# Accumulators of idle streams lent to the running ones in a four-layer graph-attention kernel

## The chip, the cores and the metric

The kernel runs on one core of a Trainium2 chip. The metric is the device time of one execution in microseconds (us); lower is better. Before the change the median of three runs is 2951.32 us (2948.66 to 2954.25).

## What is computed

The input `x` holds 32 batches of 512 nodes with 256 features, and `adj` is one 512 x 512 graph for all. Four residual layers follow each other, each with a layer norm and a relu ahead of it. Cut to what matters:

```python
def gat(h, W, a_i, a_j, alpha, mask):            # one attention
    Wh  = h @ W
    e   = leaky_relu((Wh @ a_i)[:, :, None] + (Wh @ a_j)[:, None, :], alpha)
    att = softmax(where(mask, e, -inf), axis=2)
    return att @ Wh

for layer in (0, 1, 2, 3):
    h = relu(layernorm(x))
    # 0: x += elu(gat(h, W0, alpha=0.2))           masked
    # 1: x += relu(gat(h, W1, alpha=0.01))         masked
    # 2: x += elu(gat with 4 heads of 64 features) masked
    # 3: o = relu(h @ mlp1_w + b1)                 512 features
    #    o = elu(elu(gat(o, W_fc, 0.2, no mask))) + o
    #    r = relu(o @ mlp2_w + b2)                 256 features
    #    x += relu(elu(elu(gat(r, W_hand, 0.2))) + r)
```

All of it is in fp32. The exponentials of a leaky relu of a sum factor into products, so the kernel needs no exponential of a 512 x 512 matrix: it builds `w = max(row, column) * mask` on VectorE and multiplies values that were scaled before.

## The kernel before

The 32 batches run in `NS = 4` streams: stream i works on batches i, i + 4, i + 8 and so on, one after another. A stream is a Python generator (`stream`, `batch`, `layer0` to `layer3`). Each time it has recorded a piece of work it yields the time at which its next piece may begin. The loop at L748 to L762 always runs the generator with the smallest time, so that pieces of the four streams are interleaved in the recorded program. Stream i begins `LEAD = 75` planned microseconds after stream i - 1, and each ends when its last batch is done; so only at the beginning and at the end are there fewer than four at work. A fifth generator, `setup`, prepares the mask and the projected weight columns in the same loop (L750 to L755) with the banks of the last stream.

After the recording, a scheduler puts the instructions of each engine in an order, planning with the dependences and with the buffers that each tile may use. Every engine then runs its list in that order. So a different supply of buffers can change the order on all engines, and not only waits.

TensorE's results land in the 8 accumulator banks of PSUM, each 128 x 512 fp32. `bank()` (L74) hands them out: the tag is `b` and the number of the current stream, with `8 // NS = 2` buffers per tag. `turn[0]` is the current stream, set by the loop (L756). During `setup` it is stream 3, but the mask's four transposed blocks go round the streams 3, 2 and 1 (L209). A tile of a tag waits until the tile two before it on that tag has been read by ScalarE (ACT) or VectorE (DVE).

All matmuls go through `matmul` (L66) and all transposes through `transpose` (L70), so the profile shows these two lines; the tile names tell which part it is. The users of `bank()` that the change and the prediction touch:

- `project` (L107): the projected columns of a weight (`WFC`, `WHA` and so on). Transposes into one bank, an ACT copy to `wT` (L114), matmuls of 3 columns into a second bank, and a DVE copy (L120).
- `values` (L301): four blocks of `h @ W`, each read by two ACT instructions (L312 and L313, or L315 and L318 with `both` of L317 between).
- `weights` (L336): four transposes of a column, then four DVE instructions `w` (L346, or L352 without mask).
- `averages` (L390): four matmuls `v,w` of 257 columns, a reciprocal on DVE (L380), and ACT reads (L414 and L415, L433, L692 and L693).
- `project_half` (L512): a block of the 512-wide attention's values, read by ACT (L521 and L522).
- `sort_attend` (L556): the unmasked attention by sorting, with scatters (L600), reloads (L607), prefix sums on DVE (L618 to L639) with small matmuls `before` and `after` between, a table to DRAM (L640), and gathers into two buffers `g` (L648) that L663, L667 and L668 read. `mlp_in` (L712) transposes each result `y` and adds it (L719).
- `attend` (L524): the same attention by matmuls, for batch 31 alone.
- `norm` (L256): statistics (L262, L263) and the normalised `xn` (L269 or L273), which `turn_pair` transposes and ACT copies to `hT` (L283). `add_elu` (L396) ends layers 0 and 2 with L398 and L399.

Of the kernel before, what the change touches and what calls it, by code (L numbers as in the profile page):

```python
# [19 lines left out]
FP = mybir.dt.float32  # L20
# [8 lines left out]
P = 128  # L29
# [6 lines left out]
def fast(ctx, tc, flag, x, adj, w0, a0, w1, a1, w2, a2, mlp1_w, mlp1_b, mlp2_w, mlp2_b,  # L36
         w_fc, a_fc, w_hand, a_hand, out):
    nc = tc.nc
    B, N, F = x.shape
# [6 lines left out]
    NS = 4  # L46
# [6 lines left out]
    psum = ctx.enter_context(tc.tile_pool(name="psum", bufs=1, space=bass.MemoryType.PSUM))  # L53
    dram = ctx.enter_context(tc.tile_pool(name="dram", bufs=1, space=bass.MemoryType.DRAM))

    turn = [0]
# [11 lines left out]
    def transpose(p, x, i, tied=False):  # L68
        spent[0] += 2 * P
        instruction = nc.tensor.transpose(p, x, i)  # L70
        if tied:
            tc.keep_in_program_order(instruction)

    def bank():  # L74
        return psum.tile([P, N], FP, tag=f"b{turn[0]}", name="b", bufs=8 // NS)


    nc.scalar.preload_act_table_set("natural_log_exp_and_others")
# [28 lines left out]
    def project(dst, block, k, a_cols):  # L107

        ft, n = a_cols.shape[1], a_cols.shape[2]
        p = bank()  # L110
        for f in range(ft):
            transpose(p[:, f * P:(f + 1) * P], block(k, f), ident)
        wT = work.tile([P, N], FP, tag="y", name="wT", bufs=3)
        nc.scalar.copy(wT[:, :ft * P], p[:, :ft * P])  # L114
        q = bank()
        for f in range(ft):
            matmul(
                q[:, :n], wT[:, f * P:(f + 1) * P], a_cols[:, f, :], start=(f == 0), stop=(f == ft - 1)
            )
        nc.vector.tensor_copy(dst, q[:, :n] if len(dst.shape) == 2 else q[:, :n].rearrange("p (h c) -> p h c", c=3))  # L120
# [79 lines left out]
    def setup():  # L200
# [7 lines left out]
        for j in range(NT):  # L208
            turn[0] = NS - 1 - j % (NS - 1)  # L209
            p = bank()  # L210
            for t in range(NT):
                transpose(p[:, t * P:(t + 1) * P], own[:, t, j * P:(j + 1) * P], ident, j + t == 0)
            nc.scalar.copy(maskT[:, j, :], p)
# [534 lines left out]
    while ready:  # L748
        i = min(ready, key=ready.get)
        if i == NS:  # L750
            turn[0] = NS - 1
            ready[i] += 4.0
            if next(early, early) is early:
                del ready[i]
            continue  # L755
        turn[0], spent[0] = i, 0.0  # L756
        begun[0] = ready[i]
        wait = next(streams[i], None)
        if wait is None:
            del ready[i]  # L760
        else:
            ready[i] = wait  # L762

# [409 lines left out]
@with_exitstack  # L1173
def kernel(ctx: ExitStack, tc: tile.TileContext, *args):
    nc = tc.nc
    keep = ctx.enter_context(tc.tile_pool(name="keep", bufs=1))
    flag = keep.tile([1, 1], I32, name="flag")
    fast(tc, flag, *args)
    bad = nc.values_load(flag[0:1, 0:1], min_val=0, max_val=1)
    with tc.If(bad > 0):  # L1180
        general(tc, *args)
# [27 lines left out]
```

## Time and profile before

| | |
|---|---|
| median of three runs | 2951.32 us |
| profiled execution | 2955.39 us, span 2953.7 us |
| TensorE (PE) busy | 2870.6 us, 97% |
| weight loads (PEld) | 2329.4 us, 79% |
| VectorE (DVE) busy | 2224.6 us, 75% |
| ScalarE (ACT) busy | 1538.9 us, 52% |
| GpSimd (POOL) busy | 497.2 us, 17% |
| mean TensorE clock granted | 0.994 |
| instructions | 43083 |
| DMA | 270.89 MB, 92 GB/s |

Busy times are sums over an engine's instructions. Matmuls are pipelined and their ends are modelled, so a busy TensorE need not be one at its peak; an fp32 matmul of L66 shows as two passes, a transpose of L70 as one. Lines of a timeline give the start in us, the length, the engine, the line and operation, the tiles (written <- read), and in brackets how long the engine was idle before and what released it.

### The profile page before, as it was taken

What the parts mean: (1) busy time and instruction counts of PE and PEld (TensorE: products, weight loads), DVE (VectorE), ACT (ScalarE), POOL (GpSimd) and SP (SyncE); (2) the same over time, 40 slices, a digit from 0 to 9 for tenths busy, and PEclk for the clock granted to TensorE, in tenths of its full rate; (3) what the DMA queues carried; (4) which work ended last, traced back from release to release, by engine and by line L of the source; (5) the groups of instructions that cost most, each with busy time, mean ns of one, the idle gap of its engine ahead of it and who ended that gap; (6) DMA issues with size and microseconds to landing.
All of it is one profiled execution on the core that took longest, in us unless ns stands there. A gap on an engine that the chain in (4) does not pass through costs nothing.

```text
span 2953.7 us, 43083 instructions
## 1 busy us (share of the span) xinstructions
PE 2870.6 (97%) x15177; PEld 2329.4 (79%) x15177; DVE 2224.6 (75%) x5674; ACT 1538.9 (52%) x3918; POOL 497.2 (17%) x509
## 2 busy tenths in 40 slices
PE   7999999999999999999999999999999999999998
PEld 5778888778887877888778888778878778887765
DVE  4578878778878777878778777787777788777763
ACT  3445555554555555555545555545555555555544
POOL 0011122111122121121111121111121111221120
PEclk9999999999999999999999999999999999999999
DMA  3033233233232332233332232222232322332330
GB/s 93 12 100 95 83 98 115 82 99 98 83 101 96 99 101 91 85 106 94 101 94 87 87 115 92 96 97 91 87 116 90 98 94 86 94 115 76 98 108 16
DMA packets 193150, 270.89 MB, mean 92 GB/s; under 512 B 16992, under 2 KB 156062, under 8 KB 192928
## 3 DMA queue, kind: packets, MB, share of 16 engines
q1 hardware_dynamic: 163168, 169.76, 18.4%
q0 software_dynamic: 29760, 98.30, 10.2%
q8 instruction: 123, 2.02, 0.3%
q14 instruction: 99, 0.81, 0.1%
HBM read 152.62 MB, written 115.39 MB: 91 GB/s over the span
## 4 chain that ended last, share of the span: by engine, by line
PE 80%; DVE 12%; ACT 5%; issue 1%; DMA 1%; POOL 0%; SPq 0%; POOLq 0%; ACTq 0%; DVEq 0%
PE b L66 72%; PE b L70 7%; DVE st L262 3%; DVE xn L273 1%; DVE xn L269 1%; DVE sums L634 1%; ACT v L318 1%; DVE sums L625 1%; DVE x L399 1%; ACT rs L265 1%; DVE y L398 1%; DVE mv L263 1%; DVE y L703 1%; ACT y L498 1%; ACT q L497 0%
## 5 line engine op out<-in xcount | busy, mean ns | idle before, releaser
L66 PE MATMUL b<-v,w 128*128 128x65 f32 (+1 forms) x7232 | 1221.6, 321 | 11.0 <-DVE w L346 8.5
L66 PEld LDWEIGHTS b<-v,w 128*128 128x128 f32 x7232 | 1050.1, 191 | 175.1 <-issue 66.0
L66 PE MATMUL b<-WFC,oT 128*128 128x256 f32 (+1 forms) x2048 | 499.6, 381 | 3.0 <-ACT ends L521 3.0
L66 PEld LDWEIGHTS b<-WFC,oT 128*128 128x128 f32 x2048 | 375.0, 190 | 52.0 <-ACT v L522 3.4
L66 PE MATMUL b<-W,hT 128*128 128x259 f32 (+1 forms) x1536 | 384.6, 389 | 5.0 <-ACT v L318 4.4
L346 DVE SCALAR_TENSOR_TENSOR w<-b,v,maskT 128x512 f32<-128x512 f32 x512 | 370.2, 747 | 4.6 <-PE b L70 3.4
L600 POOL DMA_INDIRECT order<-v,at x248 | 280.3, 1130 | 490.2 <-DVE oT L719 152.4
L66 PEld LDWEIGHTS b<-W,hT 128*128 128x128 f32 x1536 | 284.8, 191 | 55.7 <-ACT v L318 10.7
L346 DVE SCALAR_TENSOR_TENSOR w<-spread,v,maskT 128x512 f32<-128x512 f32 x384 | 270.1, 746 | 0.0
L380 DVE RECIPROCAL rden<-b 128x1 f32<-128x1 f32 (+1 forms) x516 | 79.6, 166 | 252.6 <-PE b L66 250.8
L706 POOL TENSOR_TENSOR x<-x,y 128x512 f32<-128x512 f32 x64 | 81.1, 1268 | 1076.3 <-ACT y L704 962.8
L66 PE MATMUL b<-hT,WM 128*128 128x512 f32 x512 | 249.1, 597 | 0.7 <-ACT hT L283 0.7
L648 POOL DMA_INDIRECT g<-table,at x124 | 121.2, 977 | 732.5 <-ACT y L668 380.9
L66 PE MATMUL b<-oT,WM 128*128 128x512 f32 x512 | 231.4, 595 | 0.0
L522 ACT ACTIVATE v<-b,ends 128x256 f32<-128x256 f32 x256 | 119.0, 468 | 179.0 <-PE b L66 174.5
L262 DVE BATCH_NORM_STATS2 st<-x 128x6 f32<-128x256 f32 x512 | 192.9, 408 | 5.2 <-DMA x<-in_x_dram 2.6
L283 ACT ACTIVATE hT<-b 128x512 f32<-128x512 f32 x256 | 147.2, 592 | 91.3 <-PE b L70 91.2
L332 ACT ACTIVATE oT<-b,bias 128x512 f32<-128x512 f32 x128 | 87.8, 686 | 195.4 <-PE b L66 195.4
L405 DVE TENSOR_TENSOR y<-q,y 128x512 f32<-128x512 f32 x192 | 132.7, 691 | 67.4 <-ACT q L404 66.5
L70 PE MATMUL b<-ident,xn 128*128 128x128 f32 x1024 | 154.9, 279 | 23.9 <-DVE xn L273 18.0
L66 PEld LDWEIGHTS b<-oT,WM 128*128 128x128 f32 x512 | 97.6, 191 | 95.8 <-issue 92.5
L70 PEld LDWEIGHTS b<-ident,xn 128*128 128x128 f32 x1024 | 125.4, 144 | 59.8 <-DVE xn L273 33.5
(142 smaller groups left out, 3749.1 us busy)
## 6 DMA issues: line engine op xcount, KB each, us to landing
table<-sums SPq DMA_DIRECT2D x62, 1032.0 KB
sums<-order SPq DMA_DIRECT2D x62, 516.0 KB
spread<-row SPq DMA_DIRECT2D x96, 256.0 KB
x<-in_x_dram SPq DMA_DIRECT2D x32, 512.0 KB
out_dram<-x SPq DMA_DIRECT2D x64, 256.0 KB
sums<-order SPq DMA_DIRECT2D x62, 129.0 KB
order<-v,at POOLq DMA_INDIRECT x248, 2.9
g<-table,at POOLq DMA_INDIRECT x124, 4.7
```

The source lines that it names most:

```text
L66: nc.tensor.matmul(p, w, x, **flags)
L70: instruction = nc.tensor.transpose(p, x, i)
L262: nc.vector.bn_stats(st[:, i, :], xt[:, t0 + i, :])
L283: nc.scalar.activation(hT[:, :, t0 * P:(t0 + 2) * P], p.rearrange("p (k n) -> p k n", k=KF), AF.Relu)
L332: nc.scalar.activation(o[:, f, :], p, AF.Relu, bias=bias[:, f:f + 1])
L346: w = nc.vector.scalar_tensor_tensor(wt[:, j, :], r, t_col(j), maskT[:, j, :], op0=OP.max, op1=OP.mult)
L380: nc.vector.reciprocal(r, den)
L405: nc.vector.tensor_tensor(r, q, r, op=OP.add)
L522: nc.scalar.activation(halves[c][:, t, :F], ps[:, :F], AF.Copy, scale=ends[:, t, 0:1])
L600: nc.gpsimd.indirect_dma_start(out=orders[c], out_offset=bass.IndirectOffsetOnAxis(ap=at[:, 0, t:t + 1], axis=0), in_=halves[c][:, t, :], ...
L648: nc.gpsimd.indirect_dma_start(out=g, out_offset=None, in_=table, in_offset=bass.IndirectOffsetOnAxis(ap=at[:, 1, t:t + 1], axis=0),)
L706: nc.gpsimd.tensor_tensor(xr, xr, y, op=OP.add)
```

## The change

`bank()` no longer uses the current stream's tag alone. A set holds the streams that have begun and not ended. The tags of all streams that are not in it are added to the current stream's own, and a counter over all calls picks one of them in turn. While all four streams are active the list holds the own tag only. During `setup`, stream 3's list starts with its own tag, and it counts as not active until it begins.

```diff
+    active = set()
+    banks = [0]
+
     def bank():
-        return psum.tile([P, N], FP, tag=f"b{turn[0]}", name="b", bufs=8 // NS)
+
+        own = [turn[0], *(i for i in range(NS) if i not in active and i != turn[0])]
+        banks[0] += 1
+        return psum.tile([P, N], FP, tag=f"b{own[banks[0] % len(own)]}", name="b", bufs=8 // NS)
@@
         turn[0], spent[0] = i, 0.0
         begun[0] = ready[i]
+        active.add(i)
         wait = next(streams[i], None)
         if wait is None:
             del ready[i]
+            active.remove(i)
         else:
             ready[i] = wait
```

No other line is changed. The number of banks stays 8, two buffers to each of four tags.

## The prediction

> **What bounds the kernel now.** I read the page's busy times first (TensorE 97% of the span), then the chain that ended last, then the busy times cut in three stretches, because the change can only act where some stream is idle: before the fourth stream has begun, and after the first has ended.
>
> ```profile
> PE 80%; DVE 12%; ACT 5%; issue 1%; DMA 1%; POOL 0%; SPq 0%; POOLq 0%; ACTq 0%; DVEq 0%
> PE b L66 72%; PE b L70 7%; DVE st L262 3%; DVE xn L273 1%; DVE xn L269 1%; DVE sums L634 1%; ACT v L318 1%; DVE sums L625 1%; DVE x L399 1%; ACT rs L265 1%; DVE y L398 1%; DVE mv L263 1%; DVE y L703 1%; ACT y L498 1%; ACT q L497 0%
> ```
>
> ```profile
> 0.00:200.00 200.00, 170.85 (x901) 139.31 (x902) 119.40 (x344) 78.11 (x210) 13.36 (x20) 0.95 0.21 65
> 200.00:2790.00 2590.00, 2556.99 (x13619) 2083.61 (x13618) 2017.33 (x5135) 1385.85 (x3540) 460.40 (x466) 1.00 0.30 95
> 2790.00:2953.70 163.70, 142.77 (x660) 106.48 (x658) 87.82 (x196) 74.90 (x168) 23.46 (x23) 0.95 0.20 64
> ```
>
> Columns of the stretches: length, busy time of PE, PE's weight loads, DVE, ACT, POOL, granted clock, DMA. The long middle is 98.7% busy at full clock. The start leaves 29.2 us of PE unused and the end 20.9 us, both at a mean clock of 0.95. Of these 50 us about 8.3 (first weights, 5.35 + 2.94) and 9.8 (after the last matmul at 2943.9) can't go, so some 32 us of gaps plus what the half clock costs is all that there is to win. The middle can't move: the changed program, built but not run, lists on every engine the same instructions in the same order with the same waits between these two zones (TensorE's order differs in its first 300 of 4,700 rows and in some 130 before its end). So the sum is over the two zones, and a time won in the first stays won, because what follows is a saturated queue in one order.
>
> Next I looked at the gaps on TensorE inside the zones, in order of time, and at what stood on the other engines then.
>
> ```profile
> 42.35 1.05 PE L66 MATMUL b<-WFCa,wT 128*128 128x3 f32 x8 [0.24 <-ACT wT L114]
> ...
> 43.44 0.17 DVE L120 COPY WFC<-b 128x3 f32<-128x3 f32 x1 [1.47 <-PE b L66]
> ...
> 43.52 0.68 DVE L399 SCALAR_TENSOR_TENSOR x<-y,x 128x512 f32<-128x512 f32 x1
> ...
> 46.24 0.16 DVE L120 COPY WFC<-b 128x3 f32<-128x3 f32 x1 [1.17 <-PE b L66]
> ...
> 48.58 0.42 PE L70 MATMUL b<-ident,xn 128*128 128x128 f32 x1
> ...
> 56.77 7.79 PE L66 MATMUL b<-v,w 128*128 128x257 f32 x32 [0.94 <-DVE w L346]
> ```
>
> The weight projections (stream 3's two banks in turn: four transposes, an ACT copy, eight passes of 3 columns, a DVE copy) run one after another, and DVE, in order, holds batch 0's layer-0 result (L399, ready when L398 ends at 41.98) behind them until 43.52, and its statistics again for 1.17 us. That stretch also pays a half clock (44 to 52 us: 0.57).
>
> ```profile
> 2837.38 2.02 PE L66 MATMUL b<-WHA,rT 128*128 128x259 f32 x8 [0.66 <-ACT v L312]
> ...
> 2842.30 0.67 PE L66 MATMUL b<-v,w 128*128 128x257 f32 x2 [2.31 <-DVE w L346]
> ...
> 2869.87 5.43 PE L66 MATMUL b<-WFC,oT 128*128 128x259 f32 x16 [2.97 <-ACT ends L521]
> ...
> 2938.02 2.00 PE L66 MATMUL b<-v,w 128*128 128x257 f32 x8 [0.69 <-ACT y L693]
> ...
> 2940.76 2.00 PE L66 MATMUL b<-v,w 128*128 128x257 f32 x8 [0.73 <-DVE y L703]
> ```
>
> Four of these five are waits for a bank to be emptied, not for data: a WHA or WFC block waits for ACT's read of the block two before it (L312, L521), an average for the last one's L693 or for L703. The 2.31 is data (w).
>
> **What the Trainium skill says.** "Perfetto Trace Analysis", Matmuls: independent groups should rotate through different banks, so that one's evacuation overlaps the next one's matmuls; the trace agrees (0.69 and 0.73 above are that overlap missing). "PSUM — Partial Sum Buffer", Specifications (TRN2): there are 8 banks, here two to each of 4 streams, so one stream alone leaves six unused. "TensorE: Matmul & The Clock Gate", What's actually happening: a quiet window of some 3.4 us halves the clock until a busy one has passed; here 0.50 to 0.62 in slices after gaps of 2.6 to 3.4 us, and 16 passes took 5.43 us where the same 16 take 3.66. So a gap of about 3 us costs up to 1.8 us more.
>
> **The change part by part.** No instruction is added or removed. A tile of `bank()` gets another of the same 8 buffers, the order planned for all engines shifts with it, and some waits go. With all four streams active the list holds the own tag alone. I follow the changed listing by hand with durations of the trace (a 257-column matmul, two passes, 0.44; a transpose 0.11; eight 3-column passes 1.0; w 0.67).
>
> *Start, to the first layer-1 average of batch 0 (56.77).* The first w (25.68) comes at about 25.4: before it stand the fourth value block, L299 and the 2.27 us of L219, unchanged; only a transpose or two is saved. From there, while four w's arrive at 0.67 each, the listing gives PE a second average and WFC transposes to do beside the first. At 28.6 remain: 11 matmuls of 0.44 (4.8), 4 of A2 (1.4), 14 transposes (1.8), four WFC projections (4.0), four xn transposes (0.5): 12.5, so 41.1, with 0.2 of waits 41.3. Before, the same point is the end of the WFCa group at 44.63 to 46.06. The WFC copies follow each other now (three in a row on ACT), so the gaps of 0.51, 0.24 and 0.73 go, and DVE reaches the second L399 some 2 us sooner. Its chain L399 0.69, statistics 1.05, xn 0.6 ends at 44.5 (46.98 before), its transposes start at 44.7 instead of 48.58, for now only one projection is ahead of them. After them 5.5 value matmuls and a projection (2.4 + 1.0), 1.2 of L315, L317, L318 and 0.9 for the first w: about 50.9, that is 5.9 earlier. The stretch has new waits of 0.45 (hT) and 1.0 (L318) in my walk, and a half clock may meet it elsewhere; I book 5.0. Ends: 0 (the chain is hidden by another) and 7.
>
> *64 to 185.* The gap of 2.65 us at 67.65 (ACT rs L265) gets two value matmuls of 268 columns in it: 0.9. The two at 104.87 and 108.98 (2.41, 1.22, data of DVE xn) get two layer-1 value matmuls and later neighbours, less a new wait for w of about 0.9: 1.0 net. The one at 176.47 (3.37 for the sorted sums' DMA) gets one more matmul: 0.4. Sum 2.3, ends 0 and 4.
>
> *End, 2834 to 2850.* The 0.66 for L312 goes, but DVE now does two xn before w, so the wait of 2.31 turns into about 3.2 with four xn transposes (0.44) inside it: +0.3 gain, ends -1 and +1.5.
>
> *2861 to 2886.* PE goes through all four WFC blocks and the first of the other half without ACT: 2.97 and up to 1.8 of half clock go, PE is at the first y at 2870.3 instead of 2875.14. Not all is kept: what is late next is the gathers. There are two g buffers; the third and fourth gather (issued 2869.06 and 2872.68) follow ACT's L668, which my walk puts no earlier, and land 4.3 to 6.0 us later. L405 of the third y stands behind the L663 of the fourth gather on DVE. So PE waits again at y 1 (1.4 us) and at y 2, and w of L352 starts at 2880.9 instead of 2882.63: 1.8. Then halves of two averages are interleaved while w's arrive at 0.67 against 0.44: 0.7. I book 2.0; ends 0.5 and 4.5.
>
> *2926 to the end.* 0.43 of the wait for rT (0.49) is filled by a WHA block; rT's transposes move up into the wait for w (0.44); two averages interleave over the w's (0.8); 0.69 and 0.73 go. Sum 3.1. The last L380, L692, L404, L405, L703, L704, L706 and the store hang on the last average and move with it. Ends 1.5 and 4.
>
> Sum: 5.0 + 2.3 + 0.3 + 2.0 + 3.1 = 12.7. I take 11 of it, since a walk sees more waits that go than waits that come. The profiled execution, 2955.39 with a span of 2953.7, would become 2944.4; the median of the runs is 2951.32, so 2940.3.
>
> **Rivals.** *The gain is absorbed (2947).* Both zones are chains of one batch through DVE, ACT and DMA, and banks only shorten PE's part. For: DVE carries 12% of the chain, the sort's DMAs set 176 and the gathers 2866 to 2882. Against: the end (3.1) hangs on nothing but banks. Only that and a third of the start: about 4.5, 2946.8; this is also the case within 0.2%, which is 5.9 us and about what a measurement of this kernel can tell from no change. *Only one zone pays:* start alone 7.3, 2944; end alone 5.4, 2946. *A new wait (2958).* Two running streams now share the idle one's banks, and a bank goes round by count, not by who is done: a stream can get a bank that another has not emptied. Places: streams 0 to 2 at 75 to 200 us, and 2 and 3 after 2800, where an average waiting for L692/L693 behind a gather on ACT (3.15 us idle at 2867) would hold PE's queue. Each costs up to 3.4 plus 1.8 of half clock. It decides when more than four such stalls come, 19 us against the 12.7. Against it: the changed listing has fewer rows of PE that wait for ACT, 67 instead of 84 in the first 300 and 28 instead of 46 in the last 140. *No effect:* excluded in the strict sense, since the orders differ.
>
> **How the numbers follow.** Full gain as booked 0.55, one zone 0.2, absorbed 0.17, new wait 0.08. Faster by over 0.2% takes the first and most of the one-zone case (7.3 is, 5.4 just isn't): 0.55 + 0.14, with part of the absorbed case near the bound: 0.76. Same 0.18, slower 0.06. The likeliest alone spans 2935 to 2945; to leave out no more than 2 in 10 the range goes up to 2948 and down to 2934 (the sum of good ends is 21, not taken in full).
>
> **What would show it.** In the changed profile: the first 128x257 matmul of layer 1 at 50 to 52 us instead of 56.77; no wait of PE for L521 near 2866, and waits for y L405 there instead; the last average's matmuls back to back after 2930; the middle stretch the same length as before to 2 us, with a span shorter by 11. Wrong would be: the layer-1 matmuls still at 56, PE waiting for L692, L693 or L313 of another stream, or a longer middle.

## The result and the profile after

The changed kernel takes 2943.4 us in the median against 2952.7 us before: a ratio of 0.9969 with a 95% interval of 0.9963 to 0.9976, that is 9.2 us less (7.1 to 10.9). The forecast was 2940.3 us, 11 us less. The profiled execution after is 2940.78 us with a span of 2939.1, so the two profiled spans differ by 14.6 us and not by 9.2. The difference between the two figures matters below: single executions of one kernel scatter by some 4 to 5 us to either side, and what the profile before showed was not all typical.

Lines of after are those of before plus 6 (plus 8 behind the loop). The chain that ended last, of after, by engine:

```profile
PE 77%; DVE 13%; ACT 5%; DMA 3%; issue 1%; POOL 0%; SPq 0%; POOLq 0%; ACTq 0%; DVEq 0%
```

Busy times of after in the same stretches (the last is shorter by the 14.6 us):

```profile
0.00:200.00 200.00, 178.89 (x936) 145.56 (x937) 123.22 (x362) 81.16 (x223) 15.99 (x22) 0.96 0.23 70
200.00:2790.00 2590.00, 2557.00 (x13622) 2083.96 (x13622) 2016.77 (x5129) 1386.47 (x3544) 459.55 (x467) 1.00 0.30 95
2790.00:2939.10 149.10, 129.42 (x622) 98.78 (x620) 84.52 (x184) 69.08 (x153) 22.05 (x20) 0.97 0.20 66
```

The middle is what it was, 2557.0 us of TensorE in 2590. In the first 200 us TensorE has 8 us more work in, and the end has 19.7 us of unused time instead of 20.9, in a stretch that is shorter.

The start and the end on TensorE, in order of time, after:

```profile
44.74 0.48 PE L70 MATMUL b<-ident,xn 128*128 128x128 f32 x1
...
51.65 7.21 PE L66 MATMUL b<-v,w 128*128 128x257 f32 x32 [0.84 <-DVE w L352]
...
2862.06 0.63 PE L70 MATMUL b<-ident,y 128*128 128x128 f32 x4 [1.06 <-DVE y L411]
2865.61 0.66 PE L70 MATMUL b<-ident,y 128*128 128x128 f32 x4 [1.20 <-DVE y L411]
...
2919.85 7.21 PE L66 MATMUL b<-v,w 128*128 128x257 f32 x32 [0.45 <-DVE w L352]
```

Layer 1 starts at 51.65 instead of 56.77. At the end all 32 matmuls of the last average run in one block of 7.21 us. All waits of TensorE from 2745 us on, after (us in total, times, the longest):

```profile
PE b L70 <- DVE y L411: 4.1, 5, 1.2
PE b L70 <- DVE xn L279: 2.1, 1, 2.1
PE b L66 <- DVE w L352: 1.8, 5, 0.8
PE b L70 <- ACT v L324: 0.5, 1, 0.5
```

The waits for a bank to be emptied (L312, L521, L693, L703 of before) are gone. What is left is data.

### The profile page after: what moved, and what is told of

Read it like the earlier page. It is cut to its first block, busy times and chain, and to the rows that moved or that the text cites. A ratio compares the mean times of both kernels' runs of the same rounds, so it can differ in the third digit from the quotient of the medians.

```text
span 2939.1 us, 43065 instructions
## 1 busy us (share of the span) xinstructions
PE 2865.3 (97%) x15177; PEld 2328.3 (79%) x15177; DVE 2224.5 (76%) x5674; ACT 1536.7 (52%) x3918; POOL 497.6 (17%) x509
## 3 DMA queue, kind: packets, MB, share of 16 engines
q0 software_dynamic: 29760, 98.30, 10.1%
## 4 chain that ended last, share of the span: by engine, by line
PE 77%; DVE 13%; ACT 5%; DMA 3%; issue 1%; POOL 0%; SPq 0%; POOLq 0%; ACTq 0%; DVEq 0%
PE b L66 70%; PE b L70 7%; DVE st L268 3%; DVE xn L279 1%; DMA order<-v,at 1%; DVE xn L275 1%; DVE sums L640 1%; ACT v L324 1%; DVE w L352 1%; DVE sums L631 1%; DMA sums<-order 1%; DVE x L405 1%; DVE mv L269 1%; DVE y L404 1%; ACT rs L271 1%
```

## The experiments

Every kernel here computes the whole result. Times are differences to the kernel before, from the ratio of the runs, with the 95% interval. The two halves were tried first.

**Only the start.** Ended streams stay in `active`:

```diff
-            active.remove(i)
```

> Banks of streams that have not begun are lent, those of ended streams are not: the first half of the change alone. Sum theory (two zones, each worth what it was booked at): the first 128x257 matmul of layer 1 at 51.5 to 52 us as with the whole change, the gap near 2866 (2.97 us for L521) back, and a median 7.3 us under the kernel before (6 to 8). Rival, one zone only: 0 to 2 us if all of the 9.3 us of the whole change comes from the end, 9 us if all comes from the start. Rival, absorbed: layer 1 starts 5 us sooner, but by 200 us less than 3 us of it is left, and so in the median.

Measured: 2.7 us less (0.9 to 4.7). Layer 1 starts at 51.74 as in the whole change, and near 2866 the old kind of wait is back:

```profile
2865.01 6.61 PE L66 MATMUL b<-WFC,oT 128*128 128x259 f32 x16 [3.01 <-ACT v L528]
```

So the mechanism is as expected and the worth isn't: 7.3 lies outside the interval, and 2.7 is what the "absorbed" case gives for the median.

**Only the end.** All streams count as begun:

```diff
-    active = set()
+    active = set(range(NS))
```

> All streams count as begun from the outset, so only banks of ended streams are lent: the second half alone. Sum theory: layer 1 at 56.8 us as before, no wait of TensorE for L521, and a median 5.4 us under the kernel before by the booking, 2 us by the difference of the whole change (9.3) and the start's booking (7.3); so 2 to 5.5. Rival, one zone only: 9 us here and nothing from the start, or 0 here. The two halves together should give 9.3 us within 1.5 if they don't touch each other.

Measured: 4.7 us less (2.7 to 6.5). With 2.7 the halves make 7.4, which agrees with 9.2 within the two intervals. That both zones pay is settled; one zone alone is excluded. Its start has the order of the kernel before, and that laid open what was wrong with the start's booking. TensorE in order of time, end only:

```profile
6.85 1.01 PE L66 MATMUL b<-W0a,wT 128*128 128x3 f32 x4 [0.87 <-DVE xn L279]
...
24.36 2.58 PE L66 MATMUL b<-v,w 128*128 128x257 f32 x8 [2.56 <-DVE w L352]
...
54.35 7.79 PE L66 MATMUL b<-v,w 128*128 128x257 f32 x32 [0.94 <-DVE w L352]
```

The same three points in the profile of before are these (its 56.77 stands in the prediction):

```profile
8.95 0.98 PE L66 MATMUL b<-W0a,wT 128*128 128x3 f32 x4 [2.94 <-DVE W0a L104]
...
26.57 3.21 PE L66 MATMUL b<-v,w 128*128 128x257 f32 x8 [2.56 <-DVE w L346]
```

One order, and 2.1 us between them from the first product on. In before, the two small loads of `W0a` came late; VectorE, in order, held the statistics of batch 0 behind the scaling of `W0a`:

```profile
7.05 0.17 DVE L105 TENSOR_SCALAR W0a<-W0a 128x2 f32<-128x2 f32 x1 [1.05 <-DMA W0a<-in_L_gnn_a_dram]
...
8.68 0.17 DVE L104 TENSOR_SCALAR W0a<-W0a 128x2 f32<-128x2 f32 x1 [1.01 <-DMA W0a<-in_L_gnn_a_dram]
```

**The changed kernel once more**, to see whether that belongs to the change:

> The changed kernel once more, beside the others of this call. The profiled executions of before and after differ by 14.6 us, the medians by 9.3. Theory, scatter in the start: in the profile of before W0a's small DMA was late (2.94 us of TensorE waiting for W0a L104), in that of the end-only kernel, which has the same order there, it was not (0.87), so some 2.4 us of the 5.1 at the first layer-1 average belong to no change. Then a second profile of the changed kernel shows either a wait of some 2.4 us before the first W0a product and layer 1 at some 54, or none and layer 1 at 51.6 to 51.9 again; and the median is 9 us under the kernel before, 7 to 11. Rival: the 5.1 us belong to the change, the median differs by 12 or more on this chip.

Measured: 8.6 us less (5.6 to 11.8). No late W0a, the first average at 24.66 and layer 1 at 51.87. A profile of the kernel with split banks (below) has the late W0a again (2.41 us), so the change doesn't remove it. It is scatter: with equal loads layer 1 gains 2.7 us (54.35 and 54.65 in two profiles with the order of before, 51.65 to 51.92 in five with the order of after), not 5.1. A sixth, at 53.82, is taken up under the half clock.

**Which banks matter at the start.** A flag lets only the projections and the mask, or only the batches, borrow (nothing is lent at the end):

```diff
+        own = own if in_setup[0] else own[:1]      # start_setup
+        own = own[:1] if in_setup[0] else own      # start_streams
```

> Start alone, and of it only the weight projections and the mask's transposes borrow banks; batch 0 to 2 keep their own, and nothing is lent at the end. By the booking the start is gained because the projections no longer run one after another through one pair of banks: then nearly all of the start's gain is here, the first layer-1 average at some 52 us (27 to 28 us after the first average of layer 0, against 30.0 without lending and 27.1 with it), and a median 2 to 3 us under the kernel before. Rival, the batch's own stages need the banks: layer 1 stays 29.5 to 30 us after the first average, median within 1 us of before.

> The reverse: batches 0 to 2 borrow the banks of streams that have not begun, the projections keep stream 3's pair, nothing is lent at the end. By the booking little is left: layer 1 at 29 to 30 us after the first average of layer 0 and a median within 1.5 us of the kernel before; waits of TensorE for wT stay. Rival: 27 to 28 us after it, and 2 to 3 us under the kernel before.

The first average of layer 0 and that of layer 1, with the projections borrowing, then with the batches borrowing:

```profile
23.85 2.58 PE L66 MATMUL b<-v,w 128*128 128x257 f32 x8 [2.35 <-DVE w L354]
...
51.31 7.79 PE L66 MATMUL b<-v,w 128*128 128x257 f32 x32 [0.94 <-DVE w L354]
```

```profile
24.27 4.56 PE L66 MATMUL b<-v,w 128*128 128x257 f32 x12 [2.46 <-DVE w L354]
...
55.79 6.56 PE L66 MATMUL b<-v,w 128*128 128x257 f32 x29 [0.84 <-DVE w L354]
```

27.5 us against 31.5, where the order of before has 30.0 and the whole change 27.1. So the projections' queue for one pair of banks is what the start pays for; more banks for the batch alone only let its average go ahead of the projections. The median doesn't show the gain, though: 0.6 us more (1.5 less to 2.7 more) for the first, where 2 to 3 less were expected, and 1.2 less (3.5 less to 1.2 more) for the second. The profile of the first reaches the block near 2790 at 2785.3, where the three with the order of before have 2788.2 to 2790.5. The clock of all runs, below, shows where the rest went.

**Half clock.** With TensorE's order kept, layer 1 still came at different times (53.82 in a kernel below, against 51.65 to 51.92), so I looked at the granted clock in slices of the start. After, then the kernel `best_split2` of below, which has the same work there in another order:

```profile
24.00:28.00 4.00, 3.47 (x11) 2.71 (x12) 3.47 (x8) 0.00 (x0) 0.34 (x1) 0.57 0.67 133
...
40.00:44.00 4.00, 3.53 (x15) 2.63 (x13) 2.15 (x6) 0.96 (x3) 0.00 (x0) 0.63 0.00 0
44.00:48.00 4.00, 3.95 (x15) 2.59 (x13) 0.75 (x4) 2.16 (x7) 0.00 (x0) 0.51 0.00 0
```

```profile
24.00:28.00 4.00, 4.00 (x26) 3.62 (x25) 3.18 (x13) 0.00 (x0) 0.93 (x1) 1.00 0.81 177
...
40.00:44.00 4.00, 3.58 (x21) 2.66 (x21) 0.85 (x6) 2.44 (x8) 0.00 (x0) 1.00 0.00 0
44.00:48.00 4.00, 2.87 (x14) 2.08 (x13) 3.09 (x7) 1.10 (x3) 0.00 (x0) 1.00 0.00 2
```

In most of 24 to 28 and 40 to 48 the first runs at half clock and loses up to 1.7 + 1.5 + 2.0 = 5.2 us by it; the second loses nothing. Up to the last matmul the half clock comes in all traces in stretches of 3.41 us or a few of them together, so each takes up to 1.7 us of work. This is the fixed window of 3413 ns that the Trainium skill gives in "TensorE: Matmul & The Clock Gate", What's actually happening. Counted from the clock's records up to the last matmul, one profiled execution each (near 200 us the first WFC block, of 8 passes, near 2790 the second, of 16; the last WHA block is the one ahead of the last average):

| kernel | first average, layer 1 | block near 200 us | half stretches to 200, from 2740 | block near 2790 to last WHA | last WHA to end |
|---|---|---|---|---|---|
| before | 26.57, 56.77 | 202.35 | 6, 3 | 135.9 | 27.3 |
| end_only | 24.36, 54.35 | 198.67 | 5, 4 | 134.9 | 24.7 |
| end_last | 24.39, 54.65 | 200.23 | 6, 2 | 134.0 | 24.7 |
| start_setup | 23.85, 51.31 | 196.92 | 5, 4 | 137.0 | 27.3 |
| start_streams | 24.27, 55.79 | 198.92 | 5, 4 | 136.7 | 26.9 |
| start_only | 24.55, 51.74 | 195.73 | 5, 3 | 137.5 | 26.9 |
| after | 24.53, 51.65 | 194.54 | 5, 1 | 131.2 | 24.7 |
| after_again | 24.66, 51.87 | 195.84 | 5, 1 | 132.4 | 25.2 |
| gathers | 24.71, 51.92 | 195.01 | 5, 1 | 129.9 | 24.7 |
| tail | 24.66, 51.78 | 195.57 | 5, 1 | 132.4 | 23.1 |
| best_shared | 25.02, 53.82 | 195.93 | 5, 4 | 134.8 | 22.7 |
| split | 25.95, 50.20 | 192.83 | 4, 2 | 133.0 | 25.1 |
| best_split2 | 23.11, 46.02 | 190.14 | 3, 2 | 133.8 | 22.8 |

Take 1.7 us per stretch (and 2.1 for the late W0a) off the block near 200: the order of before gives 190.0, 190.2 and 190.0, the change's order 186.0, 187.2, 187.3, 186.5, 187.1 and 187.4. By this estimate from single profiles the change is worth 3.1 us at the start in work and waits, and 1.1 more by the clock (5 stretches against a mean of 5.7). The middle between these blocks is 2588.0 to 2591.2 us in three profiles with the order of before and 2588.7 to 2591.8 in six with that of after: no difference beyond its scatter.

Single profiles needn't be typical (the profiled run of `start_streams` is the second slowest of its 13), but the mean granted clock of every run is on record. One minus it, times the span, is the time that half clock took from the run, an upper bound of its cost, since TensorE stands still in part of it. Means in us, against the runs of before taken beside each kernel (17.5 to 18.3 us of half clock in 111 runs):

| kernel (runs) | half clock took | against before | the rest of the time against before |
|---|---|---|---|
| after_again (8) | 15.5 | 2.0 less | 6.5 less |
| start_only (20) | 16.7 | 1.7 less | 1.1 less |
| end_only (21) | 18.3 | 0.1 less | 4.3 less |
| start_setup (21) | 20.2 | 2.8 more | 1.9 less |
| start_streams (13) | 13.2 | 4.3 less | 2.9 more |

The differences of the clock are good to 1.3 to 2.3 us, those of the rest to 1.0 (1.5 in the first row); the 20 runs of after in the result have 15.5 too. So banks for the projections do save nearly what was expected, and that order loses it again to half clock; why it meets more of it is open. Banks for the batches alone make the rest longer. The end's gain owes the clock nothing that shows, the start's seems to owe it a good part.

**Only the last stream borrows at the end.**

```diff
+        own = own if len(active) == 1 else own[:1]
```

> Nothing is lent at the start, and at the end only the very last running stream (batch 31 alone, once batch 30 is out) borrows the idle banks. The traces so far split the end so: 0.9 us up to the WFC blocks of batch 31, 2.9 from there to its last WHA block, and 2.2 in the last stage (4.35 on TensorE, of which 2.1 are given back behind the last matmul). Theory: the first two need two running streams with idle banks beside them; so here only the last stage is gained, the last average's matmuls run back to back, TensorE waits for v L528 or ends L527 near 2866 as before, and the median is 2 us under the kernel before (1 to 3). Rival: all of the end's gain (5 to 6) comes from the last stage.

Measured: 1.8 us less (0 to 3.8), and the two parts part as expected. The wait near 2866 is there and the last average is in one block:

```profile
2865.69 5.43 PE L66 MATMUL b<-WFC,oT 128*128 128x259 f32 x16 [2.75 <-ACT ends L528]
...
2927.69 7.21 PE L66 MATMUL b<-v,w 128*128 128x257 f32 x32 [0.46 <-DVE w L353]
```

**All banks in one ring, all the time.**

```diff
-        return psum.tile([P, N], FP, tag=f"b{turn[0]}", name="b", bufs=8 // NS)
+        return psum.tile([P, N], FP, tag="b", name="b", bufs=8)
```

> All eight banks in one ring for all streams, all the time (the kernel before with one tag of eight). The prediction's reason for a bounded change was that the middle is 98.7% busy and can't move, and its rival that banks which go round by count make a stream wait for another's eviction. Theory: the middle, from the WFC block near 200 us to that near 2790, takes 2590 us as in nine profiles of one order (2588.2 to 2591.8) within 4, and the ends gain about as with the change; median 5 to 10 us under the kernel before. Rival: waits of TensorE for the eviction of another stream's bank in the middle, which is then longer by 10 us or more, and the median above the kernel before.

Measured: 3420.4 us, a ratio of 1.158. My theory falls. The page of this kernel (TensorE's busy time, its clock in 40 slices) and its longest waits of TensorE:

```profile
PE 3025.5 (88%) x15177; PEld 2440.4 (71%) x15177; DVE 2263.4 (66%) x5674; ACT 1560.2 (46%) x3918; POOL 498.0 (15%) x509
...
PEclk8999999999999999999999999999999999999989
```

```profile
PE b L66 <- DVE sums L625: 92.3, 22, 4.4
PE b L66 <- issue: 82.0, 24, 6.2
PE b L70 <- DVE y L405: 79.2, 31, 5.0
PE b L70 <- DVE xn L273: 57.3, 32, 4.7
PE b L66 <- DVE oT L719: 41.2, 15, 4.4
```

The waits are listed as us in total, times, the longest. TensorE is unused for 396 us instead of 83 and busy for 155 us more, with 135 half stretches instead of 9 (up to 215 us of work). The waits shown with an engine's name are for data, up to 5 us each; in before those for xn L273 come to 18.0 us and those for y L405 to 0.6, and the other two aren't there. My reading is that one ring ties every engine's order to the order in which the streams take banks, so a stream whose sums or gathers aren't there holds the others. That the plan's order changed from the first instructions on is visible; that it is the ring's order alone is argued. So the middle could move: it didn't in the change because the lists there are the same.

**Idle banks split between the running streams**, each with a count of its own, so that none gets a bank another still fills:

```diff
+        idle = [i for i in range(NS) if i not in active and i != turn[0]]
+        running = sorted(active | {turn[0]})
+        own = [turn[0], *(t for k, t in enumerate(idle) if running[k % len(running)] == turn[0])]
```

> The change, but each idle stream's banks go to one running stream alone and each stream counts for itself, so no stream can get a bank that another one still fills. If sharing by one count costs waits (the rival of a new wait, held small): the 4.9 us in eight waits for ACT hT L289 in the first 340 us fall to some 2, and the median is 1 to 3 us under the changed kernel. If sharing is harmless, or more banks for whoever asks are worth more than the waits: within 1 us of the changed kernel, or up to 2 us slower.

Measured: 10.9 us less (6.8 to 15.1). ACT hT waits fall from 4.9 to 1.7 us, and the block near 200 comes at 183.9 and, in `best_split2`, 185.0 in the corrected count, 2 to 3 us before the change's. In the runs the two can't be told apart.

**The four gathers of batch 30 at once** (`many` is true for batch 30, and the first loop issues all four):

```diff
-            g = work.tile([P, 4 * C], FP, tag="g", name="g", bufs=2)
+            g = work.tile([P, 4 * C], FP, tag="v" if many else "g", name="g", bufs=4 if many else 2)
```

> The change as it is, and for batch 30 (the last that sorts) all four gathers are issued at once, into four buffers of the idle tag v, instead of two and then one behind each finished pair. The booking said that after the wait for L521 is gone the gathers are what is late next (waits of 1.06, 1.20 and 1.16 us for y L411 in the changed trace, at 2862, 2866 and 2870, and w of the last batch behind them). If so: two of these three waits go and the median falls by 1.5 to 2.5 us under the changed kernel. Rival, the chain behind each gather (L411's products, ACT's exp, mlp_in) sets the pace and not the landing: the waits stay, 0 to 0.5 us.

Measured: 8.0 us less (4.7 to 10.9), so no gain over the change that the runs show. TensorE's waits there:

```profile
2865.29 0.63 PE L70 MATMUL b<-ident,y 128*128 128x128 f32 x4 [0.96 <-DVE y L411]
2868.85 0.66 PE L70 MATMUL b<-ident,y 128*128 128x128 f32 x4 [1.20 <-DVE y L411]
2875.11 1.10 PE L66 MATMUL b<-v,w 128*128 128x257 f32 x4 [1.09 <-DVE w L358]
```

The first two stay: behind a landed gather the chain of DVE and ACT for each y sets the pace. The later ones shrink, and the last WHA block comes some 0.8 us sooner after the first WFC block of batch 31 (61.3, and 61.6 in `best_shared`, against 61.9 to 62.6 in three profiles with two buffers). So by the profiles two buffers cost under 1 us, not 1.5 to 2.5.

**What is given back at the very end.** In after, TensorE's last matmul is 16.6 us earlier than in before, the end of the span 14.6. Behind the last average, after, DVE and GpSimd:

```profile
2927.76 1.26 POOL L712 TENSOR_TENSOR x<-x,y 128x512 f32<-128x512 f32 x1 [11.57 <-ACT y L710]
...
2928.08 1.23 DVE L409 TENSOR_SCALAR q<-q 128x512 f32<-128x512 f32 x1 [0.17 <-ACT q L698]
```

L409 took 0.43 us in before (as L403), when GpSimd had ended its add:

```profile
2941.50 1.27 POOL L706 TENSOR_TENSOR x<-x,y 128x512 f32<-128x512 f32 x1 [13.28 <-ACT y L704]
...
2943.51 0.43 DVE L403 TENSOR_SCALAR q<-q 128x512 f32<-128x512 f32 x1 [0.54 <-ACT q L692]
```

The last batch's adds on VectorE:

```diff
-            nc.gpsimd.tensor_tensor(xr, xr, y, op=OP.add)
+            (nc.vector if b == B - 1 else nc.gpsimd).tensor_tensor(xr, xr, y, op=OP.add)
```

> The changed kernel with the last batch's x + y (L712) on VectorE instead of GpSimd, and nothing else. In the changed trace TensorE is 4.35 us quicker over the last stage, but the time from its last matmul to the end of the span grows from 9.8 to 11.8 us; of that L409 is 0.8, running 1.23 us while GpSimd's L712 of the first pair runs. Theory: L409 is 0.43 again, the last add 0.69 instead of 1.26, last matmul to end 9.8 us, and the median 1 to 2 us under the changed kernel (2943.4 to 2944.7 so far). Rival: L409 was slow for another reason (ACT's L699, which it doesn't wait for, or the L782 before it), stays at 1.2, and the median is the changed kernel's within 0.5.

```profile
2930.65 0.69 DVE L712 TENSOR_TENSOR x<-x,y 128x512 f32<-128x512 f32 x1 [0.46 <-ACT y L710]
...
2931.26 0.42 DVE L409 TENSOR_SCALAR q<-q 128x512 f32<-128x512 f32 x1
```

L409 is 0.42 again, and last matmul to end is 10.1 us instead of 11.8 (9.8 expected). The Trainium skill's "SBUF — State Buffer", Who interferes with whom, says that a `tensor_scalar` in a two-port mode and GpSimd exclude each other for a whole instruction; 1.23 against 0.42 agrees, though no trace shows the mode. It is 1.23 in all six profiles that have GpSimd's add beside it, and 0.42 or 0.43 in the other seven profiles of the table above. The runs give 9.4 us less (6.8 to 12.4), which doesn't separate it from the change.

**Versions that put this together.** `best_shared` is the change, the four gathers, the adds on VectorE and `W0a` scaled on GpSimd; `best_split2` is the split banks, the gathers and the adds:

> The change and three things that the traces point to: all four gathers of batch 30 at once; W0a scaled on GpSimd, so that the statistics behind it on VectorE don't stand behind a late small DMA; the last batch's x + y on VectorE, because the changed trace shows L409 at 1.23 us instead of 0.43 while GpSimd runs L712. Theory: 0.8 us from the gathers, 0 to 2.4 from W0a according to the execution (1 in the mean), 0.7 at the end (0.57 from the shorter add, and L409 back at 0.43): a median 2.5 us under the changed kernel, 11.5 under the kernel before. In the trace: no statistic of batch 0 later than 6 us, L409 at 0.43. Rival: none of them is on the path, within 0.7 us of the changed kernel, and L409 stays at 1.2, since it is not GpSimd that slows it.

> The change with idle banks split between the running streams (as in split), batch 30's four gathers at once, and the last adds on VectorE. By sums from the traces: 0.8 us for the gathers, 1.5 to 2 for the end, 0 to 1.5 for the split at the start: a median of 2940.5 to 2942, about 11.5 us under the kernel before and 2.5 under the changed kernel. Rival: parts cancel, as the changed kernel within 1 us.

Measured: 10.9 us less (7.1 to 15.1) and 12.7 less (8.9 to 16.5; median 2937.7 us). No W0a was late in the profile of the first, so what GpSimd does for that case is open; L409 (there L410) is 0.42 in it. The second has the quickest start of all:

```profile
23.11 2.87 PE L66 MATMUL b<-v,w 128*128 128x257 f32 x12 [2.25 <-DVE w L354]
...
46.02 7.21 PE L66 MATMUL b<-v,w 128*128 128x257 f32 x32 [0.84 <-DVE w L354]
```

Both beat the kernel before. That they beat the change isn't shown, since the intervals overlap.

## Why the prediction was right, and where it wasn't

**Where the gain lies.** Two zones, the middle unmoved, waits for banks gone, waits for y in the place of that for L521: all as said. The halves measured one by one exclude the one-zone rival. What part is due to the free banks and what to the order that was planned with them is open: no run has the one without the other.

**Start to layer 1, booked 5.0.** The trace says 5.1, but 2.1 of it is the late W0a of the profile before, a wait that the prediction counts with what can't go (2.94); the order is worth 2.7. That 5.1 stands beside the booked 5.0 is luck. The first half of the walk held: the WFC projections and the four xn transposes are done 15.7 us after the first average, where the walk has 15.0 (41.3, with the first average 0.9 behind the first w at 25.4). The step that failed is "DVE reaches the second L399 some 2 us sooner", with the xn transposes at 44.7 instead of 48.58. They came at 44.74 because everything in that execution was 2 us earlier. Counted from the first average, VectorE reaches that L399 (here L405) at 16.1 us, against 17.0 in before and 15.5 in end_only, and then it waits for a copy of the next projection, WHA, ahead of the statistics. After:

```profile
40.59 0.69 DVE L405 SCALAR_TENSOR_TENSOR x<-y,x 128x512 f32<-128x512 f32 x1
42.77 0.16 DVE L126 COPY WHA<-b 128x3 f32<-128x3 f32 x1 [1.49 <-PE b L66]
42.85 0.74 DVE L268 BATCH_NORM_STATS2 st<-x 128x6 f32<-128x256 f32 x2
```

The xn transposes stand at 20.2 us, against 22.0 and 21.1: 0.9 to 1.8 us and not 3.9. I took one execution's loads for the kernel's. Two sums of the walk are also off by some 0.3: fourteen transposes at 0.11 make 1.5 and not 1.8, and what is listed behind 44.7, with 0.4 for the four transposes, ends at 50.6 and not 50.9.

**64 to 185, booked 2.3.** From layer 1 to the block near 200: 144.3 to 145.6 us in three profiles with the order of before, 142.9 to 144.0 in five with that of after. About 1.6, inside its ends. Together the start is worth some 4.2 by the profiles where 7.3 were booked, and the runs of the start alone say 2.7 (0.9 to 4.7).

**End.** To the last WHA block 2.3 were booked (0.3 + 2.0). After, after_again and tail need 132.0 us from the block near 2790, the five kernels without lending to two streams 136.2: 4.2. But these have 2 to 4 half stretches there and the change has one, a difference of up to 2.2 x 1.7 = 3.7 us, and best_shared with four stretches needs 134.8. That the end's gain is mostly clock, as these profiles suggest, isn't borne out by the runs: end_only loses as much to half clock as before does (18.3 us each) and is 4.3 us shorter in the rest. The prediction had one such price (1.8 behind L521). So 4.2 is the least certain part.

**2926 to the end, booked 3.1.** TensorE gained 4.4 us, from 17.3 in the four profiles without lending there to 12.95, more than booked. Then some 2.0 were given back, for a net of about 2.3. The sentence that failed is "hang on the last average and move with it": moved closer, the last chain meets L710 on ACT (0.3) and GpSimd's add (0.8); the rest of the 2.0 is only that the last matmul, the flag's, no longer stands 0.85 us further behind the last average.

**Sum.** 4.2 + 4.2 + 2.3 = 10.7 by the profiles, 9.2 (7.1 to 10.9) by the runs, 11 forecast. By the profiles the start was booked 3 too high, the end 1 too low, and the 1.7 taken off covered the difference; by the runs of the halves the start was 4.6 too high and the end (4.7 against 5.4) right within its interval. So the total is right in part by luck: the flat 1.7 was taken off for no wait in particular, and errors offset each other.

**Rivals.** "Absorbed" was true for some 40% of the start by the profiles (3.1 of 7.3) and for more by the runs (4.6); up to layer 1 it is a chain through DVE, as its text has it. "A new wait" was put at 5.2 us for each stall and at few stalls; no stall of that size came: the changed kernel's eight waits for hT in the first 340 us make 4.9 us, none over 0.8 (before has three, 1.2 us). The pooled kernel shows what it costs when all streams share: 467 us. The prediction's reason for a fixed middle, its being saturated, was too weak; the identical lists were the reason that held.

## What to carry to other kernels

Before a stage is priced from one trace, find in it what belongs to that execution alone: late small loads and stretches of half clock moved the same list of instructions by 2 to 4 us here, up to half of the change's worth. Lend accumulators of idle streams where a stage runs alone, above all to work that queues for one pair (the weight projections), but measure it, since the order that comes of it can lose its gain to the clock, and don't let all streams draw from one ring. When TensorE's last stage is shortened, look at what follows its last matmul: engines that used to be apart now meet.

## What the runs showed of the hardware

A gap of TensorE of 2.73 us before the first average was followed by half clock within the next 8 us in all six profiles that have it, one of 2.46 or 2.56 us in three of four, and one of 2.25 or 2.35 us in none of three. The Trainium skill's "TensorE: Matmul & The Clock Gate", What's actually happening, asks for an idle window of about 3.4 us; here half clock followed shorter gaps. Where a gap falls tells more than its length: in each profile all half stretches begin on one grid with steps of 3.41 us (within 0.03 us). Over all fourteen profiles, from 6 us to the last matmul, half clock followed 110 of the 111 steps of that grid in which TensorE stood for 2.0 us or more, 38 of 79 with 1.4 to 2.0 us, and 83 of 11932 with less. The gap of 2.56 us in end_only fell into two steps (1.04 and 1.52 us) and had no half clock behind it; in before 2.06 of the same gap fell into one.

The changed kernel also got half clock from 41 us on, with no gap above 0.5 us in the 4 us before, while TensorE ran the projections' matmuls of 3 columns among others, and again from 75 us, behind matmuls of 65 columns; what sets that off was not tried.

One order on TensorE can get different counts. Up to layer 1, five profiles of the change's start have three stretches of half clock and `best_shared` four; the split banks have one in one profile and none in the other. So part of the scatter of single executions comes in steps of 1.7 us.
